# Where in the on-chip memory the operands of three aggregations start: tiles moved to multiples of 512 bytes

## The chip, the cores and the metric

The kernel runs on one core of a Trainium2 chip. The metric is the device time of one execution in microseconds; the time of a kernel is the median of several executions. Beside it stands one execution taken by the hardware profiler, from which all the views are made.

## What is computed

Four graph layers follow each other on 2708 nodes with 512 features, each in the form x = x + layer(relu(layernorm(x))), all with one adjacency matrix of zeros and ones. Cut to what matters:

```
# layer 0
support = a.T @ h;  out = relu((support @ weight) * in_degree ** -0.5)
# layer 1: the first 64 neighbours of every row
keep = (A > 0) & (cumsum(A > 0, axis=1) <= 64)
xj = leaky(keep @ h / cnt @ W_nb.T + b_nb);  out = leaky(h @ W_line.T + b_line) + xj
# layer 2: 8 heads of graph attention, softmax over the neighbours
# layer 3
agg = mask @ h / deg
out = relu(concat(h @ W_self + b_self, agg @ W_nb + b_nb) @ W_comb + b_comb)
```

Layers 0, 1 and 3 hold a plain aggregation: the (masked) adjacency matrix times a matrix of 2708 x 512. Layer 2 weighs its neighbours and is computed in another way.

## The kernel before

**Tiling.** The nodes lie in 22 chunks of 128 (the last has 20). In each of the three plain layers a dense stage first normalizes a chunk, transposes it and multiplies it by a weight matrix (line 186, in fp32), and `halves` (lines 290 to 312) splits the product into two parts, a rounded value and the remainder, both of type float32r. A part is 128 x 512 elements of 4 bytes, 2048 bytes in each partition; the two of a chunk lie one after the other. They are kept for all chunks in a ring of 21 tiles `halves` and one shorter tile `tail`, in the pool `ring` for layers 0 and 1 (line 473) and `ring3` for layer 3 (line 1439). Layers 0 and 1 take their ring from the same place, one after the other.

**The aggregation.** For a span of three or four (in places two) chunks of output columns and each of the 22 chunks m of rows, a tile of adjacency values is made as float32r: `ar` in layer 0, by ScalarE (line 548), `kt` in layer 1, by VectorE (line 846), `kt3` in layer 3, by VectorE from bytes (line 1491; the profile calls both of these `kt`). Then `matmuls` runs, for every chunk of the span, one or two matmuls:

```python
            nc.tensor.matmul(
                acc[:R],
                weight[:, k * R : (k + 1) * R],
                parts[:, i, :],
```

So a 128 x 128 slice of the adjacency tile (512 bytes in each partition) is the stationary operand, and a whole part of `halves` is streamed: 946 matmuls of 512 columns a layer, all recorded at line 423. Layers 1 and 3 use the function `aggregate`, in which the weights are made two units ahead and the accumulators of a span are evicted while the next span runs. Layer 0 has its own loop (line 718), in which the first chunks' aggregation is interleaved with the dense stage, and later the steps of a product of two weight matrices (`Fusion`, lines 362 and 369) stand between the units.

**Where tiles lie.** The program places tiles in the SBUF by pools. Pools that are opened on the left are stacked from the bottom, pools with `side="right"` from the top, which is at byte 229,344 of a partition (448 x 512 - 32). A tile's size is rounded up to a multiple of 32 bytes. A pool that is closed gives back its place. The program that is built from this kernel holds these start offsets (bytes in each partition, and modulo 512):

| layer | streamed tile | modulo 512 | stationary tile | modulo 512 |
|---|---|---|---|---|
| 0 | `halves`, 141280 + 4096 k; `tail`, 227296 | 480 | `ar`, 77312 + 2048 k | 0 |
| 1 | the same | 480 | `kt`, 135136 + 2048 k | 480 |
| 3 | `halves`, 122944 + 4096 k; `tail`, 208960 | 64 | `kt3`, 215008 + 2048 k | 480 |

The dense stages have their weight matrices at 19968 and 28160 and their transposed chunks `hT` at 52736 and 54784, all at 0 modulo 512. In attention (lines 1042 and 1242) the four buffers of `t2` start at 96, 192, 288 and 384 modulo 512, and `tails_row` at 448.

**Names that the change touches.** `const` is the first pool on the left; it holds small constants, among them `eps` (line 133) and `limit` (line 144), one float each in every partition. `eps` is the bias of the square root in `norm` (line 222), `limit` that of the sign in layer 0 (line 597). On the right lie `ring`, then the pool `l1` with `kt`; later `l2p`, `tails`, `e3` (layer 2 and the way to layer 3), and `l3` with `kt3` (lines 1485 to 1490). `ring3` is on the left, behind the pool `late`, where attention's pool `att` was until line 1435. The function `general_layers` computes the same without the assumptions of the fast path; it is run only if a test at the end of `fast_layers` asks for it, and has an `eps` of its own.

Of the kernel before, what the change touches and what calls it, by code (L numbers as in the profile page):

```python
# [8 lines left out]
F32 = mybir.dt.float32  # L9
# [11 lines left out]
P = 128  # L21
# [23 lines left out]
def fast_layers(  # L45
# [72 lines left out]
    const = ctx.enter_context(tc.tile_pool(name="const", bufs=1))  # L118
# [11 lines left out]
    nc.gpsimd.memset(oneb, 1.0)  # L130
    ones = const.tile([P, 1], F32, name="ones")
    nc.gpsimd.memset(ones, 1.0)
    eps = const.tile([P, 1], F32, name="eps")
    nc.gpsimd.memset(eps, EPS)

    deg = const.tile([P, NC], F32, name="deg")
# [4 lines left out]
    nc.gpsimd.memset(squares, 0.0)  # L141
    signs = const.tile([P, NC, len(groups)], F32, name="signs")
    nc.gpsimd.memset(signs, 0.0)
    limit = const.tile([P, 1], F32, name="limit")
    nc.gpsimd.memset(limit, NEIGHBORS - 0.5)
    index = const.tile([P, NC], F32, name="index")
    nc.gpsimd.iota(
# [1288 lines left out]


    with ExitStack() as stack:
        ring = stack.enter_context(tc.tile_pool(name="ring3", bufs=NC - 1, reuse_waits="tile"))
        b3 = ring.tile([P, D], F32, name="b3", bufs=1)  # L1440
        nc.sync.dma_start(
# [107 lines left out]
def general_layers(  # L1549
# [44 lines left out]
    const = ctx.enter_context(tc.tile_pool(name="const", bufs=1))  # L1594
# [6 lines left out]
    make_identity(nc, ident_bf)  # L1601
    ones = const.tile([P, P], F32, name="ones")
    nc.gpsimd.memset(ones, 1.0)
    eps = const.tile([P, 1], F32, name="eps")
    nc.gpsimd.memset(eps, EPS)
    deg = const.tile([P, NC], F32, name="deg")
    nc.gpsimd.memset(deg, 0.0)
# [62 lines left out]
    with tc.tile_pool(name="l0c", bufs=1) as cp, tc.tile_pool(name="l0w", bufs=2) as wk, tc.tile_pool(  # L1670
        name="l0acc", bufs=1, space=PSUM
# [124 lines left out]
    with tc.tile_pool(name="l1c", bufs=1) as cp, tc.tile_pool(name="l1w", bufs=2) as wk, tc.tile_pool(  # L1796
        name="l1acc", bufs=1, space=PSUM
# [42 lines left out]
    with tc.tile_pool(name="l2c", bufs=1) as cp:  # L1840
# [12 lines left out]
        with tc.tile_pool(name="l2p", bufs=1) as pp, tc.tile_pool(name="l2pw", bufs=2) as wk, tc.tile_pool(  # L1853
            name="l2pps", bufs=2, space=PSUM
# [57 lines left out]
        with tc.tile_pool(name="l2w", bufs=1) as wk, tc.tile_pool(  # L1912
            name="l2acc", bufs=2, space=PSUM
# [159 lines left out]
    with tc.tile_pool(name="l3h", bufs=1) as hp3, tc.tile_pool(name="l3c", bufs=1) as cp, tc.tile_pool(  # L2073
        name="l3w", bufs=1
    ) as wk, tc.tile_pool(name="l3acc", bufs=1, space=PSUM) as pacc, tc.tile_pool(
        name="l3ps", bufs=1, space=PSUM
# [56 lines left out]
def kernel(tc: tile.TileContext, *args: bass.AP):  # L2133

    nc = tc.nc
    with tc.tile_pool(name="verdict", bufs=1) as pool:
        verdict = pool.tile([1, 1], I32, name="verdict")
        fast_layers(tc, *args, verdict)
        odd = nc.values_load(verdict[0:1, 0:1], min_val=0, max_val=P + 1)
        with tc.If(odd > 0):  # L2140
            general_layers(tc, *args)
# [32 lines left out]
```

## Time and profile before

| what | us |
|---|---|
| median of 3 runs | 1770.46 (1767.06 to 1771.25) |
| the profiled execution, its own time | 1771.37 |
| its span, from the first to the last instruction | 1769.6 |
| mean granted clock of TensorE | 0.994 |

The stages of the span:

| stage | from, us | to, us |
|---|---|---|
| layer 0, dense stage and first aggregation | 15 | 125 |
| layer 0, the other aggregations | 125 | 356 |
| layer 1, dense stage | 387 | 517 |
| layer 1, aggregation (the last part beside layer 2's first chunks) | 517 | 740 |
| layer 2, dense stage and attention | 740 | 1365 |
| layer 3, dense stage | 1365 | 1540 |
| layer 3, aggregation | 1540 | 1762 |

How to read the views: PE is TensorE's matmuls, PEld its weight loads, DVE VectorE, ACT ScalarE, POOL GpSimd. A group of instructions has line, engine, operation, output<-inputs, shape and count, then busy time in us and mean ns of one, then the idle time of the engine before them and what ended it. Matmuls are pipelined: one that is recorded with 393 ns overlaps the next, so the cost of one in a row is the distance from start to start, which is also what the chain of waits gives (length by count). In a line of the stages view the columns are: stretch, its length, busy time and number of instructions of PE, PEld, DVE, ACT and POOL, then the granted clock, the share of the DMA engines and GB/s.

### The profile page before, as it was taken

How to read it: one execution, taken by the hardware profiler on the slowest of the kernel's cores; microseconds unless marked ns; L12 is line 12 of the kernel's file. 1: busy time of each engine (PE TensorE's matmuls, PEld its weight loads, DVE VectorE, ACT ScalarE, POOL GpSimd, SP SyncE). 2: the span in 40 equal slices, each digit the busy share in tenths (PEclk: the TensorE clock that was granted, in tenths of full speed). 3: DMA queues.
4: the chain of work that ended last, by engine and by line, in shares of the span. 5: the costliest groups of instructions: out<-in, count | busy, mean ns of one | idle time of the engine just before them, and what ended most of it. 6: DMA issues, size and time to landing. Idle time of an engine off the chain costs nothing.

```text
span 1769.6 us, 29469 instructions
## 1 busy us (share of the span) xinstructions
PE 1737.1 (98%) x11280; PEld 1040.0 (59%) x11280; DVE 1307.7 (74%) x1889; ACT 848.6 (48%) x1547; POOL 249.1 (14%) x252
## 2 busy tenths in 40 slices
PE   8999999999999999999999999999999999999998
PEld 4567777744458887644464544433434455588786
DVE  8649888955555556878799999999999777533334
ACT  5447666722210000265888888888794566400000
POOL 1003323311111112255000000000001222100000
PEclk9999999999999999999999999999999999999999
DMA  8436665445551111333520221121022444322221
GB/s 294 139 94 208 202 200 181 144 105 129 121 140 49 48 48 54 115 123 101 126 63 15 60 63 45 27 64 61 13 74 74 134 137 138 93 65 79 73 71 41
DMA packets 167227, 177.37 MB, mean 100 GB/s; under 512 B 84127, under 2 KB 106591, under 8 KB 166060
## 3 DMA queue, kind: packets, MB, share of 16 engines
q1 hardware_dynamic: 144428, 131.99, 27.0%
q10 hardware_dynamic: 18808, 33.37, 5.1%
q0 software_dynamic: 3840, 10.03, 1.4%
q8 instruction: 90, 1.47, 0.4%
q14 instruction: 61, 0.50, 0.1%
HBM read 111.64 MB, written 55.36 MB: 94 GB/s over the span
## 4 chain that ended last, share of the span: by engine, by line
PE 80%; DVE 10%; issue 4%; DMA 2%; ACT 2%; SPq 1%; POOL 1%; ACTq 0%; DVEq 0%; POOLq 0%
PE acc L423 34%; PE av L1242 15%; PE nb_ps L186 7%; DVE t L1042 6%; PE sums L1242 4%; PE h_ps L186 4%; PE self_ps L186 4%; PE line_ps L186 3%; PE wh_ps L186 3%; PE hT_ps L244 2%; PE fused_ps L369 1%; DVE cum L554 1%; DMA ai<-in_adj 1%; PE av_ps L1195 1%; ACT b L1060 1%
## 5 line engine op out<-in xcount | busy, mean ns | idle before, releaser
L1042 DVE SCALAR_TENSOR_TENSOR t<-rb,ec,vT 128x2708 f32<-128x2708 f32 (+2 forms) x214 | 511.0, 2451 | 17.1 <-PE sums L1242 15.6
L423 PE MATMUL acc<-halves,kt 128*128 128x512 f32 x1848 | 432.2, 393 | 2.4 <-DVE kt L846 2.1
L1242 PE MATMUL av<-t,whs 128*32 128x451 f32 (+5 forms) x4432 | 429.5, 514 | 4.4 <-DVE t L1042 1.4
L423 PEld LDWEIGHTS acc<-halves,kt 128*128 128x128 f32 x1848 | 345.2, 188 | 85.9 <-DVE kt L846 7.0
L1060 ACT ACTIVATE b<-t,eb 128x2708 bf16<-128x2708 f32 (+1 forms) x119 | 285.1, 2396 | 36.6 <-DVE t L1042 36.5
L1242 PEld LDWEIGHTS av<-t,whs 128*32 128x32 f32 (+1 forms) x4432 | 161.5, 110 | 187.4 <-issue 148.1
L423 PE MATMUL acc<-halves,ar 128*128 128x512 f32 x924 | 248.6, 419 | 1.9 <-ACT ar L548 1.9
L423 PEld LDWEIGHTS acc<-halves,ar 128*128 128x128 f32 x924 | 173.4, 189 | 63.5 <-issue 22.4
L222 ACT ACTIVATE ln_rs<-ln_mv,eps 128x1 f32<-128x1 f32 x88 | 25.5, 293 | 319.8 <-DVE ln_mv L220 312.0
L846 DVE SCALAR_TENSOR_TENSOR kt<-lastr,index,vT 128x512 fp32r<-128x512 int16 (+3 forms) x154 | 112.5, 742 | 75.8 <-PE acc L423 75.3
L1491 DVE CAST kt<-vT 128x512 fp32r<-128x512 uint8 (+3 forms) x154 | 56.6, 369 | 137.2 <-PE acc L423 137.2
L1209 POOL TENSOR_SCALAR z<-y 128x512 f32<-128x512 f32 x22 | 44.1, 2003 | 645.0 <-DMA aT<-avT 520.8
L554 DVE TENSOR_TENSOR_SCAN cum<-ai,deg 128x512 int16<-128x512 int32 (+2 forms) x110 | 130.7, 1196 | 0.0
L597 ACT ACTIVATE cum<-cum,limit 128x512 int16<-128x512 int16 (+3 forms) x132 | 88.0, 667 | 49.5 <-DVE deg L562 47.6
L218 DVE BATCH_NORM_STATS2 ln_st<-x 128x6 f32<-128x512 f32 x88 | 60.3, 687 | 51.9 <-DMA x<-x 38.1
L1027 ACT ACTIVATE whs<-wh,ef 128x64 f32<-128x64 f32 x214 | 72.8, 344 | 52.5 <-PE sums L1242 18.5
L1242 PE MATMUL sums<-t,whs 128*32 128x325 f32 (+4 forms) x952 | 91.6, 448 | 0.0
L186 PE MATMUL nb_ps<-wfn,hT 128*128 128x512 f32 x168 | 77.4, 604 | 2.1 <-ACT hT L246 2.1
L186 PE MATMUL h_ps<-w0s,hT 128*128 128x512 f32 x168 | 75.8, 594 | 0.6 <-ACT hT L246 0.6
L186 PE MATMUL wh_ps<-w2s,hT 128*128 128x512 f32 x168 | 75.9, 594 | 0.3 <-ACT hT L246 0.3
L186 PE MATMUL self_ps<-wfs,hT 128*128 128x512 f32 x168 | 75.6, 592 | 0.0
L186 PE MATMUL nb_ps<-wn,hT 128*128 128x512 f32 x168 | 75.6, 592 | 0.0
(210 smaller groups left out, 1900.3 us busy)
## 6 DMA issues: line engine op xcount, KB each, us to landing
x<-x SPq DMA_DIRECT2D x105, 256.0 KB
ai<-in_adj SPq DMA_DIRECT2D x84, 256.0 KB
x<-x ACTq DMA_DIRECT2D x84, 256.0 KB
x<-in_x SPq DMA_DIRECT2D x42, 256.0 KB
rb<-rT SPq DMA_DIRECT2D x7, 1354.0 KB
wh<-whd SPq DMA_DIRECT2D x63, 96.0 KB
packed<-two POOLq DMA_DIRECT2D x44, 128.0 KB, 3.2
whd<-wh SPq DMA_DIRECT2D x21, 256.0 KB
```

The costliest lines, as they stand in the source:

```text
L186: nc.tensor.matmul(po[:n], lhsT[:, f, :n], w[:, f, :], start=(f == 0), stop=(f == NF - 1))
L218: nc.vector.bn_stats(st[:n], xc[:n])
L423: nc.tensor.matmul(acc[:R], weight[:, k * R : (k + 1) * R], parts[:, i, :], start=(m == 0 and i == 0), stop=(m == NC - 1),)
L554: nc.vector.tensor_tensor_scan(cum[:n, :gw], ai[:n, :gw], ai[:n, :gw], 0.0 if g == 0 else deg[:n, m : m + 1], op0=ALU.add, op1=ALU.max,)
L597: nc.scalar.activation(cum[:n, :gw], cum[:n, :gw], AF.Sign, bias=limit[:n], scale=-1.0, accum_out=signs[:n, m, g : g + 1],)
L846: nc.vector.scalar_tensor_tensor(by_chunk(kt, cs), lastr[:, cs[0] * R : (cs[-1] + 1) * R].rearrange("p (c r) -> p c r", r=R), index[:R, m ...
L1027: nc.scalar.activation(t[:q, :O], wh.pop((u, m))[:q], AF.Copy, scale=by)
L1042: ins = nc.vector.scalar_tensor_tensor(t[:q, : hi - lo], row[h][:q, lo:hi], ec[:q, m, h : h + 1], vT[g][:q, k, lo:hi], op0=ALU.max, op1=AL ...
L1060: nc.scalar.activation(b[:q, : hi - lo], weight[s][:, : hi - lo], AF.Sigmoid, bias=eb[:q, m, h : h + 1], scale=STEEP,)
L1209: nc.gpsimd.tensor_scalar(z, y, 0.0, None, op0=ALU.min)
L1242: nc.tensor.matmul(p[j * S : (j + 1) * S, : b - a], lhsT, rhs[:, part * size + a : part * size + b], start=(s % NC == 0), stop=(s % NC == ...
L1491: nc.vector.tensor_copy(by_chunk(kt, cs), pattern(m, cs))
```

## The change

Only places of tiles change; no instruction is added or taken away.

```diff
@@ fast_layers
-    eps = const.tile([P, 1], F32, name="eps")
+    eps = const.tile([P, 16], F32, name="eps")[:, :1]
     nc.gpsimd.memset(eps, EPS)
...
-    limit = const.tile([P, 1], F32, name="limit")
+    edge = ctx.enter_context(tc.tile_pool(name="edge", bufs=1, side="right"))
+    limit = edge.tile([P, 120], F32, name="limit")[:, :1]
     nc.gpsimd.memset(limit, NEIGHBORS - 0.5)
...
     with ExitStack() as stack:
+        margin = stack.enter_context(tc.tile_pool(name="margin", bufs=1))
+        margin.tile([P, 112], F32, name="margin")
         ring = stack.enter_context(tc.tile_pool(name="ring3", bufs=NC - 1, reuse_waits="tile"))
@@ general_layers
-    eps = const.tile([P, 1], F32, name="eps")
+    eps = const.tile([P, 16], F32, name="eps")[:, :1]
     nc.gpsimd.memset(eps, EPS)
```

`limit` becomes the first column of a tile of 480 bytes that is the first on the right-hand side. `eps` becomes the first column of a tile of 64 bytes, so that `const` keeps its size. `margin` is a tile of 448 bytes ahead of `ring3`; nothing reads or writes it.

## The prediction

> **What bounds the kernel now.** I read the page first, then the chain of waits that ended last in order of time, then the groups by line and form, then the stages. From the page, the engines' busy time and the shares of the chain:
>
> ```profile
> PE 1737.1 (98%) x11280; PEld 1040.0 (59%) x11280; DVE 1307.7 (74%) x1889; ACT 848.6 (48%) x1547; POOL 249.1 (14%) x252
> PE 80%; DVE 10%; issue 4%; DMA 2%; ACT 2%; SPq 1%; POOL 1%; ACTq 0%; DVEq 0%; POOLq 0%
> ```
>
> TensorE holds 80% of the chain, and its line 423 (the plain aggregations) alone 34% of the span. The change moves addresses only, so the question is what one matmul of line 423 costs in each layer. The chain in order of time has start, length and count:
>
> ```profile
> 164.76 3.73 PE acc L423 x16
> 168.49 0.86 PE fused_ps L369 x2
> 327.89 22.63 PE acc L423 x96
> 517.12 185.03 PE acc L423 x814
> 1540.20 102.86 PE acc L423 x440
> 1643.18 108.72 PE acc L423 x465
> 1754.43 7.98 PE acc L423 x33
> ```
>
> The same instruction, in the same shape, has two prices. In layer 1 it is 185.03 / 814 = 227.3 ns apiece, in layer 3 102.86 / 440 = 233.8 and 108.72 / 465 = 233.8. In layer 0 the runs are cut up: 16 take 3.73 us (233.1), and 96 take 22.63 (235.7, with one short stop in it). From the single start times in the trace, the distance between two matmuls back to back is, once settled, 226, 227, 227 repeating in layer 1 (226.7 on average), 231, 232, 237 repeating in layer 3 (233.3), and 232, 235 alternating in layer 0 (233.4). The groups by form:
>
> ```profile
> L423 PE MATMUL acc<-halves,kt 128*128 128x512 f32 x1848 | 432.2, 393 | 2.4 <-DVE kt L846 2.1
> L423 PE MATMUL acc<-halves,ar 128*128 128x512 f32 x924 | 248.6, 419 | 1.9 <-ACT ar L548 1.9
> L423 PEld LDWEIGHTS acc<-halves,kt 128*128 128x128 f32 x1848 | 345.2, 188 | 85.9 <-DVE kt L846 7.0 <-DVE kt L1491 1.6 <-issue 0.4
> L1242 PE MATMUL av<-t,whs 128*32 128x451 f32 x2016 | 236.0, 542 | 1.7 <-DVE t L1042 1.4
> L1242 PE MATMUL av<-tails_row,tails_w 120*32 120x451 f32 x96 | 11.4, 542 | 0.0
> ```
>
> There is next to no idle time before these matmuls: they wait for each other. A weight load takes 188 ns and lies inside the matmul before it. And in the stages view, ACT has 0.7 us of work in layer 1's aggregation and none in layer 3's, with DMA at a share of 0.19 and 0.20:
>
> ```profile
> 517.00:705.00 188.00, 188.00 (x830) 155.07 (x829) 116.32 (x154) 0.71 (x2) 30.31 (x19) 1.00 0.19 58
> 1540.00:1770.00 230.00, 222.34 (x950) 177.20 (x948) 85.31 (x214) 0.00 (x0) 0.00 (x0) 0.99 0.20 63
> ```
>
> The slower layer 3 is the quieter one (DVE 85 us against 116), so a neighbour's traffic doesn't explain it. What differs and stays constant through a layer are the addresses. The matmul streams `halves` and loads `ar` or `kt`. Modulo 512 bytes they start, by the table of addresses above, at 480 and 0 in layer 0, at 480 and 480 in layer 1, at 64 and 480 in layer 3. Modulo 64 that is (32, 0), (32, 32) and (0, 32): the two layers whose operands differ by 32 cost 233.3, the one where they agree costs 226.7.
>
> **What the Trainium skill says.** "TensorE: Matmul & The Clock Gate", section "Back-to-back issue gap", gives N / 2.4 + 2.5 ns, about 216 for 512 columns. No layer reaches it: 11 and 17 ns more are paid. The same page, section "Step-by-step: what each phase is for", says that the array has two independent SBUF read ports, so that loading the next weights takes nothing from the running matmul. If the layers differ by their addresses, this trace shows the two reads do touch. "SBUF — State Buffer", section "Specifications (TRN2)", counts 16-byte lines; all starts here, before and after, are multiples of 32, so by that page nothing should change. Its section "Operand start alignment" treats legality and says that its runs timed nothing. The pages thus give a floor (216) and no price; the price is taken from the layers.
>
> **The change part by part.** *Instructions:* none is added or removed. The tile `margin` is never written or read, `limit` and `eps` get the same one-column memsets, and the edit in `general_layers` lies in a branch that isn't taken. Cost 0.
>
> *Addresses.* In the left-hand pool `const`, `eps` takes 64 bytes for 32 and `limit` gives back 32, so everything behind it stays: `ar` remains at 0. On the right, 480 bytes of `limit` come first, so all of the right-hand stack slides down 480: `ring` and `kt` go from 480 to 0, `kt3` from 480 to 0. In layer 3 `margin` pushes `ring3` up 448: 64 becomes 0. All three layers are then at (0, 0).
>
> *Price of (0, 0).* The trace has no matmul of line 423 there. Nearest row: layer 1, equal offsets, 226.7. I take it for all layers. Below it the floor is the page's 216; above it see the rivals.
>
> *Layer 3.* 935 of the distances are back to back, in runs of 32, 439 and 467. After a stop layer 1 needs about nine matmuls to settle (235, 233, 236, 224, 231, 236, 228, 233, 231, then 227), on average 232. So (935 - 27) x 6.67 ns = 6.1 us off, all on the chain: it is PE from 1540.2 to 1762.4 but for 1.8 us of DVE's casts and additions near 1752. Next in line is the cast of `kt3`, 427 ns for each eight matmuls (1.81 us), so nothing new becomes late.
>
> *Layer 0.* The runs are short: 7 or 8 matmuls up to 126 us, then mostly 16 between the two of line 369 (0.86 us). A run of 8 never settles: nothing. A run of 16 saves about 11 ns in its first nine and 5 x 6.6 in the rest, 44 ns; some twenty of them give 0.9 us. The longer ones (22 to 61) give (length - 9) x 6.6 ns, together some 1.5 us. Sum 2.4 us. From 181 to 243 us the chain is held by DVE's scans, ACT and loads of `ai`, where 0.7 us of it would be saved beside the chain. I take 2.0, with 1.5 and 2.4 as ends.
>
> *Layer 1.* Stays at 226.7: 0.
>
> *Other tiles moved.* `e3` (aT, sT, y, z), `l2p` and `tails` slide by 480, to other offsets modulo 64. The fp32 matmuls stream at about half the rate (line 186 takes 429 ns for 512 columns in the chain); `t2` and `tails_row` have different offsets and both take 542 ns (shown above), so I take 0, and 1 us either way for the range. DVE's and ACT's writes to `kt`, `kt3` and `halves` move by 32 modulo 64: they lie beside the matmuls (0.87 us of DVE per unit of 1.81 us in layer 1), and would have to double to be seen.
>
> *Waits by reuse.* `ring3` is 448 bytes further into the memory that attention frees, so slot 3 of `halves` now meets the end of attention's row buffer, read last by DVE's last weight there. It is written for the fourth chunk, three steps of some 8 us later: 0. The right-hand pools keep their places against each other.
>
> Sum: 6.1 + 2.0 = 8.1 us off. The profiled execution took 1771.37 (span 1769.6 and 1.8 around it), 0.9 over the median of the runs; against that, 1763.3, and for the median 1770.46 - 8.1 = 1762.4. I say **1762**.
>
> **Rivals.** *Alignment is worth more.* If starting at an odd 32 bytes costs layer 1 a step too, (0, 0) lies one more step of 6.7 ns lower, at 220: layer 1 saves 916 x 6.67 = 6.1 (all its back-to-back distances, as counted in the trace), layer 3 12.3, layer 0 2.0 + 640 x 6.67 = 6.3 (those outside 181 to 243 us). Together 25 us: 1745. For it: layer 1 still pays 11 ns over the page's 216. Against: no two rows show it. The floor itself would give about 36 us.
>
> *Slower: the offsets don't cancel, they add.* Let each operand have its own price and the odd start be the cheap one. Layer 1 has both odd (226.7), layers 0 and 3 one each (233.3), so none odd costs 233.3 + 233.3 - 226.7 = 240.0. Then layer 1 loses 860 x 13.3 = 11.5 us (its settled distances, in runs of 61, 109 and 717), layer 3 935 x 6.7 = 6.2, layer 0 some 640 x 6.7 = 4.3: plus 22, 1792. A milder form, in which (0, 0) is just not the good state and all sit at 233.3, costs layer 1's 860 x 6.67 = 5.7 us: 1776. It decides from a settled distance of about 230.6 on, where layer 1's loss (860) eats the gain of layers 3 and 0 (some 1,250 settled distances). For it: three rows can't refute a sum. Against: an aligned start dearer than a crooked one on both reads would be odd, while a clash of two reads that depends on their difference needs one assumption.
>
> *The addresses aren't the cause.* Something else that stays fixed in a layer sets the rhythm (the order of accumulators, how a run locks in): 1770. For it: layer 1 itself changes rhythm after each stop. Against: 717 matmuls in a row at 226.7, and 439 and 467 at 233.3.
>
> **How the numbers follow.** Equal offsets count: 0.51 (1762). Alignment worth more: 0.18 (1745). Not the cause: 0.13 (1770). Slower: 0.18 (half 1776, half toward 1792). The range 1744 to 1777 leaves out the lower part of the second case (0.06) and the upper half of the last (0.09), and holds the microsecond or two of the small terms. About 0.3% (5.3 us) is what a measurement can tell from no change: faster 0.46 + 0.18 = 0.64, the same 0.05 + 0.13 = 0.18, slower 0.18.
>
> **What would show it.** Layer 3's chain at 227 ns per matmul (440 in 99.9 us, for 102.86), layer 1's at 227.3 as before (814 in 185), layer 0's runs of 16 at 3.68 to 3.70 us, and `kt` and `halves` records of line 423 alike in both layers. Wrong if layer 1 leaves 226.7 in either direction, if layer 3 stays at 233.8, or if the time moves in a stage without line 423.

## The result, and the profile after

The changed kernel takes **1763.07 us** (median of 6 runs, 1759.59 to 1765.0) against 1770.14 for the kernel before in 6 runs (1767.06 to 1771.49). The ratio is 0.9957, with a 95% interval of 0.9946 to 0.9968: faster by 0.43%. The forecast was 1762. The profiled execution took 1762.76, of which 1761.0 are the span. The medians of these six runs each are 7.1 us apart, the two profiled executions 8.6; forecast were 8.1.

The chain of waits in order of time, of the changed kernel (start, length, what; its line 424 is line 423 of before):

```profile
163.86 3.67 PE acc L424 x16
167.54 0.86 PE fused_ps L370 x2
513.60 185.01 PE acc L424 x814
1537.98 99.96 PE acc L424 x440
1638.07 105.66 PE acc L424 x465
1746.28 7.79 PE acc L424 x33
```

Layer 3's two long runs fell from 102.86 to 99.96 us and from 108.72 to 105.66, so one matmul from 233.8 to 227.2 ns, stops included. Layer 0's run of 16 fell from 3.73 to 3.67, and layer 1's long run stayed (185.03 before). The groups by form of the same kernel:

```profile
L424 PE MATMUL acc<-halves,kt 128*128 128x512 f32 x1848 | 426.3, 390 | 3.5 <-DVE kt L847 3.2
L424 PE MATMUL acc<-halves,ar 128*128 128x512 f32 x924 | 246.2, 417 | 2.4 <-ACT ar L549 2.2
L424 PEld LDWEIGHTS acc<-halves,kt 128*128 128x128 f32 x1848 | 345.1, 188 | 81.4 <-DVE kt L847 8.6 <-DVE kt L1494 1.6 <-issue 0.4
```

And the stages view, its last stage:

```profile
1540.00:1770.00 230.00, 213.99 (x941) 175.43 (x939) 83.02 (x207) 0.00 (x0) 0.00 (x0) 0.99 0.20 63
```

The weight loads still take 188 ns each. The recorded duration of a matmul hardly shows the gain (393 to 390 ns, 419 to 417), because it overlaps with its neighbours; it is the distance from start to start that fell. From the single start times in the two traces (a settled distance is the mean from start to start once a run of matmuls has found its rhythm):

| | before | after |
|---|---|---|
| layer 0, mean distance in its six groups, ns | 232.6 to 233.2 | 227.5 to 230.2 |
| layer 1, settled distance | 226.67 | 226.67 |
| layer 3, settled distance | 233.33 | 226.67 |
| last matmul on `halves` in layer 0's aggregation starts at, us | 354.18 | 351.93 |
| first matmul of layer 1's aggregation | 516.88 | 513.36 |
| first matmul of layer 3's aggregation | 1540.13 | 1537.91 |
| last matmul on `halves` in layer 3's aggregation | 1761.77 | 1753.45 |

So 2.2 us come from layer 0, 6.1 from layer 3. Between the two the lead grew to 3.5 and shrank again. That is scatter of single executions: experiment 2 below, which leaves layers 0 and 1 as they were, has the first three of these points 1.5 us later, at the same time, and 1.3 us later than the kernel before. Within layer 3's aggregation there is next to no scatter: from first to last start it takes 221.6 us in the kernel before and in experiment 3, 215.5 in the changed kernel and 215.6 in experiment 2.

### The profile page after: what moved, and what is told of

It is laid out like the page before. It is cut to its first block, busy times and chain, and to the rows that moved or that the text cites. A ratio compares the mean times of both kernels' runs of the same rounds, so it can differ in the third digit from the quotient of the medians.

```text
span 1761.0 us, 29469 instructions
## 1 busy us (share of the span) xinstructions
PE 1729.5 (98%) x11280; PEld 1055.1 (60%) x11280; DVE 1307.4 (74%) x1889; ACT 849.1 (48%) x1547; POOL 249.2 (14%) x252
## 4 chain that ended last, share of the span: by engine, by line
PE 84%; DVE 10%; DMA 2%; ACT 2%; issue 1%; POOL 0%; SPq 0%; ACTq 0%; DVEq 0%; POOLq 0%
PE acc L424 32%; PE av L1243 19%; PE nb_ps L187 8%; PE sums L1243 5%; DVE t L1043 4%; PE h_ps L187 4%; PE self_ps L187 4%; PE line_ps L187 4%; PE wh_ps L187 3%; PE hT_ps L245 2%; DVE cum L555 2%; PE fused_ps L370 1%; DMA x<-x 1%; PE av_ps L1196 1%; PE adj_sums L1342 1%
## 5 line engine op out<-in xcount | busy, mean ns | idle before, releaser
L424 PE MATMUL acc<-halves,kt 128*128 128x512 f32 x1848 | 426.3, 390 | 3.5 <-DVE kt L847 3.2
L1243 PEld LDWEIGHTS av<-t,whs 128*32 128x32 f32 (+1 forms) x4432 | 171.1, 110 | 178.4 <-issue 140.4
```

The costliest lines, as they stand in the source:

```text
L424: nc.tensor.matmul(acc[:R], weight[:, k * R : (k + 1) * R], parts[:, i, :], start=(m == 0 and i == 0), stop=(m == NC - 1),)
L1243: nc.tensor.matmul(p[j * S : (j + 1) * S, : b - a], lhsT, rhs[:, part * size + a : part * size + b], start=(s % NC == 0), stop=(s % NC == ...
```

## The experiments

My theory at the outset, called **D64**: a matmul of the aggregation is cheap when its streamed tile and its weight tile start at the same offset modulo 64 bytes. The rivals: the two must agree modulo 512 (**D512**), or it is being a multiple of some power of two that counts. Offsets below are modulo 512, written (streamed, weights).

**1. Without the tile `margin`.** Layers 0 and 1 at (0, 0), layer 3 at (64, 0).

```diff
-        margin = stack.enter_context(tc.tile_pool(name="margin", bufs=1))
-        margin.tile([P, 112], F32, name="margin")
```

> The changed kernel without the tile margin: layers 0 and 1 stay at (0, 0), in layer 3 the halves go back to 64 modulo 512, with kt3 at 0. Theory D64 (the price of a matmul of the aggregation depends on the difference of the two start offsets modulo 64 bytes): the difference is 64, so layer 3 settles at 226.7 ns and the median stays at about 1763. Rival D512 (the two must be equal modulo 512, or both multiples of 512): layer 3 goes back to 233.3 ns and the median to about 1769.

Measured: 1765.81 us, ratio to the kernel before 0.9966 (0.9955 to 0.9978). The chain of layer 3:

```profile
1540.63 100.94 PE acc L424 x440
1641.69 106.67 PE acc L424 x465
```

100.94 / 440 = 229.4 ns with its stops, and 228.89 settled: a third rate that neither theory had, so both missed. D64 as it stood is in doubt, and so is a simple yes or no.

**2. Layer 3 alone, with both tiles at an odd offset.** The kernel before, and 416 bytes ahead of `ring3`: layer 3 at (480, 480), an odd multiple of 32 bytes.

```diff
+        margin = stack.enter_context(tc.tile_pool(name="margin", bufs=1))
+        margin.tile([P, 104], F32, name="margin")
         ring = stack.enter_context(tc.tile_pool(name="ring3", bufs=NC - 1, reuse_waits="tile"))
```

> The kernel before with one tile of 416 bytes ahead of ring3: layers 0 and 1 as before, in layer 3 halves and kt3 both at 480 modulo 512, so both at 32 modulo 64. D64 and D512 (a difference of zero is enough): layer 3 settles at 226.7, the median falls by about 6.1 us to 1764. Rival (multiples of 512, or at least of 64, are what counts): layer 3 stays at 233.3, the median at 1770.

Measured: 1764.44 us, 0.9968 (0.9956 to 0.9981).

```profile
1541.54 99.96 PE acc L423 x440
1641.62 105.68 PE acc L423 x465
```

To 0.02 us the two runs of the changed kernel. No tile of layer 3 is at a multiple of 64, let alone 512. Equal offsets are enough; multiples of 512 are not what counts.

**3. Layer 0 alone.** The changed kernel with a margin of 32 bytes: layers 0 and 1 at (0, 0), layer 3 at (96, 0).

```diff
-        margin.tile([P, 112], F32, name="margin")
+        margin.tile([P, 8], F32, name="margin")
```

> The changed kernel with a margin of 32 bytes instead of 448: layers 0 and 1 at (0, 0), layer 3's halves at 96 and kt3 at 0. D64: layer 3 at 233.3 (difference 32 modulo 64), and only layer 0's part of the gain is left: some 2.2 us, a median of about 1768. D512 says the same of layer 3. If layer 0's earlier end is given back before the end (its lead over the kernel before shrank from 3.5 to 2.1 us within layer 1), the median is 1769 to 1770.

Measured: 1769.34 us against 1771.0, 0.9992 (0.9983 to 1.0001). Layer 3 is back at the price of before, to within a hundredth:

```profile
1538.42 102.86 PE acc L424 x440
1641.40 108.71 PE acc L424 x465
```

In its trace layer 0's last matmul starts 3.0 us and layer 3's last 1.8 us before those of the kernel before. The median says 1.7 us less, but the interval touches no change: layer 0's part is about 2 us in the traces and not shown by the times alone. Inside layer 0 the gain itself is firm: the second of its six groups takes 47.79 us from first to last start in the kernel before and in experiment 2, and 47.11 in the changed kernel and in every experiment with layer 0 at (0, 0).

**4. A sweep of the weights' offset, near zero.** In layers 1 and 3 the weight tile starts at another offset in every span; the streamed tiles stay at 0 (layer 1) and, with a margin of 480 bytes, at 32 (layer 3). Layer 1's `kt` has the same edit as `kt3`:

```diff
-            kt = wk.tile([R, WG], F32R, name="kt3", bufs=3)
+            o = (0, 16, 32, 48, 64, 96, 0)[spans.index(cs)] // 4
+            kt = wk.tile([R, WG + 128], F32R, name="kt3", bufs=3)[:, o : o + WG]
```

> The changed kernel in which the weight tile of layers 1 and 3 starts, span by span, at 0, 16, 32, 48, 64, 96 and 0 bytes within its buffer; the halves lie at 0 modulo 512 in layer 1 and at 32 in layer 3. D64: in layer 1 the settled distance is 226.7 at offsets 0 and 64, 233.3 at 32 and 96; in layer 3 the other way round, 233.3 at 0 and 64, 226.7 at 32 and 96. At 16 and 48 open: if lines of 16 bytes are what clashes, 226.7 or 233.3 as they fall; if the clash grows with the difference, something between. D512: only offset 0 gives 226.7 in layer 1, and only 32 in layer 3.

The chain within single spans of layer 1, for offsets 16 and 32, and of layer 3 for 16:

```profile
553.99 37.63 PE acc L424 x166
593.00 38.73 PE acc L424 x166
1583.30 38.32 PE acc L424 x169
```

They are 226.7, 233.3 and 226.7 ns apiece: 16 bytes more or less than the stream cost nothing, 32 do. At 48 and 64 layer 1 was at 233.3. **D64 falls**: a difference of 64 is no better than one of 32.

**5. The sweep far from zero.** Streamed tiles at 0 in both layers; the edit as above, with other offsets, on the changed kernel with its margin of 448 bytes. Of this sweep, the one before it and experiment 6 there is one execution each, so their times say little; the spans within the trace are compared.

> The changed kernel (halves at 0 in layers 1 and 3) with the weight tile starting, span by span, at 128, 256, 384, 448, 192, 0 and 0 in layer 1 and at 320, 224, 288, 160, 480, 416 and 496 in layer 3. D64 has fallen with the first sweep (offset 64 gave 233.3). Theory now: only the difference of weights minus halves modulo 512 counts, it is cheap within 16 bytes of zero, and what happens far from zero is open. If the memory repeats every 128 bytes, 128, 256 and 384 settle at 226.7 and 160, 288 and 416 at 233.3. If it repeats at 512 only, 496 (16 below zero) settles at 226.7, 448 (64 below) at 228.9 as in the kernel without the margin, 480 and 416 at 233.3, and the offsets in the middle at 233.3 or at a rate of their own; one under 226.7 would be a better place than the changed kernel's.

Within spans of layer 1, for weights at 128, 256 and 448:

```profile
515.42 38.73 PE acc L424 x166
555.78 37.42 PE acc L424 x165
634.33 38.23 PE acc L424 x167
```

233.3, 226.8 and 228.9 ns. An offset of 256 is as good as none, so **D512 falls** too. All settled distances of the float32r runs with full weight loads, ordered by the difference weights minus stream modulo 256:

| difference modulo 256 | seen at (streamed, weights) | ns |
|---|---|---|
| 0 | (0, 0), (480, 480), (32, 32), (0, 256) | 226.7 |
| 16 | (0, 16), (32, 48) | 226.7 |
| 240, that is -16 | (32, 16), (0, 496) | 226.7 |
| 192, that is -64 | (64, 0), (0, 448), (0, 192) | 228.9 to 229.1 |
| 128 | (0, 128), (0, 384) | 233.3, 232.4 |
| 32, 48, 64, 96 | (480, 0), (0, 32), (32, 64), (0, 288), (0, 48), (0, 64), (32, 96), (0, 320), (0, 96) | 233.2 to 233.4 |
| 160, 224 | (96, 0), (64, 480), (0, 160), (0, 416), (32, 0), (0, 480), (0, 224) | 233.3 |

One function of the difference, which repeats every 256 bytes, fits every place that was tried but one: 128 and 384 are 256 apart and differ by 0.9 ns, in some 158 distances each. So the period of 256 is a good description, not an exact law. No place was under 226.7.

The weights are also written at the moved place, by VectorE in layers 1 and 3. A clash with these writes isn't the cause: in the kernel before, the distances in the first long run of layer 3 are 233.33 ns in the mean while VectorE works (189 of them) and 233.35 while it doesn't (217).

**6. A shorter weight load.** In layer 3 most matmuls use only the first 32, 64 or 96 columns of the weight slice; the stream stays 512 columns long. The output rows of the other columns get only the first and the last of their products, so the kernel leaves out a part of the layer. The weight tile lies at 0 in one span of each width and at 32 in the other.

```diff
+            n = R if (m == 0 and i == 0) or m == NC - 1 else cols
             nc.tensor.matmul(
-                acc[:R],
-                weight[:, k * R : (k + 1) * R],
+                acc[:n],
+                weight[:, k * R : k * R + n],
```

> Leaves out part of layer 3's aggregation: most matmuls take only the first 32, 64 or 96 columns of the stationary slice (spans 0 and 1: 32, spans 2 and 3: 64, spans 4 and 5: 96, span 6: all 128), so the output is wrong in most rows; the stream stays at 512 columns. The weight tile lies at 0 in the even spans and at 32 in the odd ones. Theory: the surplus over 216 ns is a clash of the next weight load with the running stream. Then it shrinks with the load: near 216 to 220 at 32 columns for both offsets, between at 64 and 96, and the difference between offsets 0 and 32 (6.7 ns at 128 columns) shrinks too. Rival: the surplus belongs to the stream itself (its start offset, its lines): 226.7 and 233.3 at every width.

The loads are shorter as intended (columns as above):

```profile
L425 PEld LDWEIGHTS acc<-halves,kt 128*64 128x64 f32 x328 | 44.0, 134 | 31.1
L425 PEld LDWEIGHTS acc<-halves,kt 128*32 128x32 f32 x328 | 35.6, 108 | 41.0
```

But the chain within the spans with 32 columns, weights at 0 and at 32, has

```profile
1536.42 38.68 PE acc L425 x167
1576.94 38.08 PE acc L425 x159
```

231.6 and 239.5 ns apiece, more than with 128 columns. With 64 columns the means are 230.1 and 231.7, with 96 columns 230.1 and 229.0. Both sides of the expectation missed: at offset 0 every shorter load costs more than the full one (226.7), at offset 32 those of 64 and 96 columns cost less (233.3) and that of 32 more. In the trace, the load of 32 columns ends 120 to 130 ns before the next matmul starts, that of 128 columns some 40, and it still costs more. So the surplus doesn't simply grow with the time that load and stream share. Yet it does depend on where the weights lie, since only they moved within the sweeps.

**7. Two-byte operands in layer 3.** The changed kernel with `halves` and `kt3` as bfloat16 in layer 3.

```diff
-            kt = wk.tile([R, WG], F32R, name="kt3", bufs=3)
+            o = (0, 32, 64, 128, 0, 0, 0)[spans.index(cs)] // 2
+            kt = wk.tile([R, WG + 256], BF16, name="kt3", bufs=3)[:, o : o + WG]
...
-            h3[c] = halves(ring, pn, c)
+            h3[c] = halves(ring, pn, c, BF16)
```

> The changed kernel with layer 3's halves and adjacency weights as bfloat16 instead of float32r, so a value is kept to some 16 bits by its two parts, and fewer bytes are read for each column; the weight tile starts at 0, 32, 64, 128, 0, 0 and 0 bytes, span by span. Theory: the surplus over 216 ns (10.7 at a difference of zero, 17.3 elsewhere) comes from two reads of 4-byte elements meeting in the memory; with 2-byte elements both reads are half as long, the settled distance is about 216 at every offset, layer 3 saves another 935 x 10.7 ns = 10 us, and the median is about 1753. Rival (the surplus belongs to the array or to its accumulators and only its size follows the offsets): 226.7 at offset 0, more at 32 and 64, a median of 1763.

Measured: 1753.44 us, 0.9904 (0.9887 to 0.992). The groups of line 427 hold both kinds side by side (some matmuls of layer 3 are missing from this trace: 905 of 924 are recorded here):

```profile
L427 PE MATMUL acc<-halves,kt 128*128 128x512 f32 x924 | 214.2, 391 | 2.3 <-DVE kt L850 2.1
L427 PE MATMUL acc<-halves,kt 128*128 128x512 bf16 x905 | 200.3, 379 | 1.5 <-DVE kt L1498 0.2
L427 PEld LDWEIGHTS acc<-halves,kt 128*128 128x128 f32 x924 | 172.2, 188 | 42.1 <-DVE kt L850 7.0
L427 PEld LDWEIGHTS <-kt 128*128 128x128 bf16 x946 | 92.1, 98 | 113.0 <-DVE kt L1498 2.3 <-issue 0.4
```

The loads halve, and the settled distance is 215.83 ns at all four offsets, 0, 32, 64 and 128. The surplus is gone, and with it the dependence on the place, at these four.

**8. Two-byte operands everywhere, at the places of before.** The kernel before with `halves`, `ar`, `kt` and `kt3` as bfloat16, and none of the moved tiles: (480, 0), (480, 480) and (64, 480). Other lines follow the type; one of them lets layer 0's small sums (line 625 of before) read `ar` element by element.

```diff
-                ar = wk.tile([R, WG], F32R, name="ar", bufs=10)
+                ar = wk.tile([R, WG], BF16, name="ar", bufs=10)
...
-            kt = wk.tile([R, WG], F32R, name="kt", bufs=3)
+            kt = wk.tile([R, WG], BF16, name="kt", bufs=3)
...
-            kt = wk.tile([R, WG], F32R, name="kt3", bufs=3)
+            kt = wk.tile([R, WG], BF16, name="kt3", bufs=3)
```

> The kernel before, its pools as they were, with the halves and the adjacency weights of all three plain layers as bfloat16 (two parts keep some 16 bits of a value); the start offsets differ modulo 64 in layers 0 and 3, as before. Theory: with 2-byte operands the offsets don't matter and every matmul of the aggregations settles at 216: layer 3 saves 935 x 17.5 = 16.4 us, layer 1 860 x 10.8 = 9.3, layer 0 some 640 x 17 = 10.9 where TensorE is the bound: a median of about 1736, up to 1745 if VectorE or the loads become the bound in layers 0 and 1. Rival (offsets still count, layer 3 of the run before was only fast because both start at multiples of 64): layers 0 and 3 stay well above 216, a median over 1750.

Measured: **1735.69 us**, 0.9796 (0.978 to 0.9812), faster than both. The ratio is to the kernel before as it ran beside it, 1772.23 us. The chain, a run of layer 0, then layer 1's long run, then layer 3:

```profile
151.97 3.45 PE acc L426 x16
507.62 147.64 PE acc L426 x684
1520.87 95.07 PE acc L426 x440
1616.06 100.48 PE acc L426 x465
```

That is 215.8 ns in layer 1 (147.64 / 684) and 216.1 in layer 3 (95.07 / 440), stops and all, and 215.6 in layer 0. Layer 0's aggregation ends 10.0 us earlier than before, layer 1's another 9.5, layer 3's another 16.6.

## Why the prediction was right

**What bounds the kernel.** Right. The chain was read as matmul after matmul of one line with two prices, and when the higher price fell the end came by as much. Nothing took its place: VectorE's casts stay far behind in layer 3 (83 us of work in the last stage).

**The addresses as the cause.** Right, and shown: experiments 1 to 5 change only places, and layer 3's price goes to 226.7, 228.9 or 233.3 with them; in the two sweeps it changes from span to span within one execution. The rival "the addresses aren't the cause" is out.

**The reading modulo 64.** Wrong in its form. Three layers gave three pairs of offsets, and I read them modulo 64, where two pairs differ by 32. What counts is the difference modulo 256, cheap within 16 bytes of zero: layer 0's differs by 32, layer 3's by 160. The forecast didn't suffer, because (0, 0) has the difference zero in either reading: that is owed to the target that was chosen, and not to the reading. For a change that had put layer 3 at (64, 0) the modulo-64 reading would have missed by about 2 us (experiment 1).

**Price of (0, 0).** 226.7 was taken from layer 1 and 226.67 came. The rival of added prices (240.0) and the one of a further step down (220) are both out, since the price depends on the difference, which layer 1 already had at zero. The prediction's floor of 216 ns was misread: the section that it names gives this figure for an isolated matmul and a lower one for a stream (see the last section). As measured, no float32r place came under 226.67.

**Layer 3.** Forecast 6.1 us; the lead over the kernel before grows from 2.22 to 8.32 us within the layer, by 6.1.

**Layer 0.** Forecast 2.0 (1.5 to 2.4), measured 2.25 at its last matmul. The sum fits better than its parts. A run of 16 saved 0.06 us for the forecast 0.044. The 17 short runs up to 122 us, put at nothing, fell from 232.4 to 230.4 ns in the mean, some 0.2 us together. From 181 to 243 us the chain runs through VectorE, before and after, as the prediction had it. The third group of matmuls, which lies there, did fall from 47.74 to 47.11 us, but the fourth, which stops for a scan, did not gain: 51.70 us before, 52.02 after, and 50.8 to 53.0 in the experiments with layer 0 at (0, 0). That scatter of 2 us is as large as the whole forecast, so part of the agreement is luck.

**Layer 1 and everything else.** Forecast 0. Layer 1's settled distance is 226.67 in both. The moved tiles of `e3`, `l2p` and `tails` and the shifted `ring3` left no trace that is larger than the scatter.

**What stays open.** That two reads meet is the likely story, for only the difference of two addresses matters and 2-byte operands end it. It is argued, not shown: no run kept a weight slice for several matmuls, which would take the load away. Experiment 6 contradicts the simple form of it, in which the cost grows with the length of the load. Nor do the runs tell whether it is the 2 bytes or the other type that ends it. Why the pattern repeats at 256 bytes, why 128 and 384 differ nonetheless, why -64 is a place of its own, and which of the two operands has to be bfloat16 was not settled; the last was not tried.

## What to carry to other kernels

When one instruction has two prices in stages that differ in nothing else, look at where its operands start. For float32r matmuls of this shape with a weight load each, place the streamed and the stationary tile at the same offset modulo 256 bytes; an alignment to 512 is not needed. Before tuning places, ask whether the operands may be bfloat16: here that was worth 2.0%, the places 0.4%. It keeps fewer bits of each value, some 16 in two parts, and that has to be allowed by the task.

## What the runs showed of the hardware

- A float32r matmul of 128 x 128 by 512 with its own weight load takes 226.67, about 228.9 or 233.3 ns from start to start, by the difference of the start offsets of its two operands; 232.4 was seen at one place, (0, 384). The bfloat16 one takes 215.83 at every place tried.
- "TensorE: Matmul & The Clock Gate", section "Back-to-back issue gap" of the Trainium skill, gives about 216 ns for 512 columns as the gap of an isolated matmul: the bfloat16 matmuls meet it with a load each (215.83), the float32r ones don't. The same section has about 131 ns for each pair of load and matmul in a sustained stream; no run here came under 215.83.
- The section "Step-by-step: what each phase is for" of the same page of the Trainium skill says that loading the next weights takes no read bandwidth from the running matmul. In bfloat16 nothing here speaks against it. In float32r the distance depends on where the weights lie (226.67 to 233.33 ns), so load and stream don't look independent there.
- After a stop a float32r run at (0, 0) mostly needs six to ten matmuls to fall into its rhythm of 226.67 ns; with bfloat16 the first distance is at most 227, and those after it 215 or 216.
- A weight load of 128 columns takes 188 ns in float32r and 98 in bfloat16; one of 32 float32r columns takes 108.
